# A four-layer network on one core: the convolution loop and the MLP on queries, with routing, put in the order of written tables, and the last group of queries in two halves

## The chip, the cores and the metric

The kernel runs on one core of a Trainium2 chip. Its engines are TensorE (PE), VectorE (DVE), ScalarE (ACT), GpSimd (POOL) and SyncE (SP); each works through its own queue in order, and semaphores tie the queues together. The metric is the device time of one execution in microseconds (us), the median of several runs; lower is better.

## The reference, cut to what matters

Four layers follow each other on 4096 tokens (8 sequences of 512) of 128 values, each on a layer norm of its input and added back to it:

```
x = x + conv(layernorm(x))      # running mean per sequence, 31 softmax weights per head and position, sum of 31 shifted copies, projection, norm
x = x + ffn(layernorm(x))       # block-quantised gated MLP, 128 -> 352 -> 128
x = x + ttt(layernorm(x))       # q, k, v; two steps of training of (gate, val, proj) on k, v; then the MLP on q:
                                #   o = (silu(q @ gate) * (q @ val)) @ proj @ proj_w + proj_b
x = x + moe(layernorm(x))       # 8 experts of 128 -> 512 -> 128, best 2 per token, at most 1229 tokens for an expert
```

For each token and each of its two choices, `moe` counts how many choices before it went to the same expert; that is its place, and a token beyond the last place is dropped for that choice. All first choices count ahead of all second ones.

## The kernel before

Tokens lie on the 128 partitions: 32 tiles of 128 tokens, in 8 groups of 4 tiles (512 tokens). Everything is float32, and a float32 matmul runs as two passes on PE. A scheduler puts the instructions of each engine in order by the order in which the program issues them and by what they depend on; where a program passes instructions through a `Line`, that engine keeps them in just the order of the calls.

**The convolution** (`sequence_conv`, 0 to 245 us) takes one sequence at a time, in a software pipeline over `cur`, `nxt`, `then` and `old` (this sequence, the next two and the one before). DVE, PE, ACT and part of POOL are passed through one `Line` each. The parts:

- `gate` and `tap`: matmuls `eg` and `ev` from the running means; ACT makes `sg` of `eg`. `energy`: two DVE operations, `en` and the running maximum `top`. `turn_top`, `greatest`, `turn_greatest`: `top` is turned on PE (`tt`), reduced on DVE (`mx`), widened on ACT (`mw`), turned back (`mb`); `less` takes it off the energies (DVE), and `weigh` makes the exponentials on ACT, a copy in PSUM (`w`) and one in SBUF (`en`) for each of four groups of taps.
- `part_sums`, `sums`, `invert`, `turn_inverse`: the softmax's sums by matmul (`pn`), a copy (`dn`, ACT), matmul (`sm`), reciprocal (DVE, L448), widened (`rw`, ACT), turned on PE (`rb`) and copied out (`rbs`, ACT). `tt`, `mb`, `pn`, `sm`, `rb` and the means `av` share one PSUM buffer.
- `shared` (POOL) and `product` (DVE, L483) multiply the weights with the shifted means, `add_up` sums them on PE (`cv`, L492), 8 matmuls for each of four groups.
- `scale_down`, `project`, `norm1`, `finish`, `add_beta`: scaling on DVE (`cs`), projection on PE (`pj`), statistics on DVE and the root on POOL, then ACT and POOL. `scaled` normalises the tokens of a later sequence (ACT), `means` makes its running means (PE, ACT, DMA).

The order in which the loop calls these parts is the order on every engine.

**The feed-forward part, training and Newton-Schulz** (245 to 930 us) are not touched.

**The MLP on queries and routing** (the last part of `ttt`, and `Moe.route`; 931 to 1057 us). For each group: `pa` and `pb`, eight matmuls of 512 columns into four PSUM buffers; Silu on ACT (`sw`); product on DVE (`ht`, L1317); the 32 output passes on PE (`o`, L1323); and the sum with the residual on DVE (`x`, L1327). `moe.route(g - 1)` is issued between a group's products and its outputs. It turns `x` on PE (`tp`, copied by ACT to `xt`), takes the statistics and a reciprocal root of 13 small DVE operations (statistics at L1671 and L1672, the root at L87 to L95), makes logits on PE (`both`, L1678), scales them (`lg`), picks the best two experts with DVE operations of 128x32 and smaller, counts places with two matmuls against a triangle and ones (`both`, L1715 and L1716), and ends with the row number `slot` (L1727) of each choice. Nothing here goes through a `Line`: the scheduler interleaves the group's products, the group before and its routing. Then POOL scatters rows to DRAM with eight indirect DMAs (L1732), one for each tile and choice: the second choices first, then the first choices, each of which waits until the second choices of the group before have landed, since second choices fill an expert's rows from the end and a first choice must win where they meet.

**The experts** (`Moe.experts`, 1058 us to the end) load their rows from DRAM (SP, L1787 and L1788) once all scatters have landed. Their first instruction on PE is the turn `tp` at L1816, their first activation a Gelu (L1834), for which ACT loads a table.

Of the kernel before, what the change touches and what calls it, by code (L numbers as in the profile page):

```python
# [1 line left out]

# [5 lines left out]
F32 = mybir.dt.float32  # L8
# [8 lines left out]
P = 128  # L17
# [112 lines left out]
def flat(ap):  # L130
    return ap.rearrange("p a b -> p (a b)")
# [17 lines left out]
def sequence_conv(cx):  # L149
# [20 lines left out]
    BUSY = 14  # L170
    with ExitStack() as st:
# [430 lines left out]
        add_up(cur, 3)  # L602
        for b in range(1, B):
            cur, nxt, then, old = seq[b], seq.get(b + 1), seq.get(b + 2), seq.get(b - 1)
            shared(cur)
            product(cur, 0)
            if b > 1:
                finish(seq[b - 2], nc.gpsimd)
            part_sums(cur)
            sums(cur)  # L610
            if old:
                scale_down(old)
                project(old)
            add_up(cur, 0)
            if nxt:
                for g in (2, 3):
                    energy(nxt, g)
            invert(cur)
            if nxt:
                turn_top(nxt)  # L620
            if then:
                gates(then, 0)
            product(cur, 1)
            if nxt:
                greatest(nxt)
            turn_inverse(cur)
            if then:
                taps(then, 0)
            if nxt:
                turn_greatest(nxt)  # L630
            add_beta(b)
            add_up(cur, 1)
            if old:
                norm1(old, nc.gpsimd)
            if b + 4 < B:
                scaled(b + 4)
            if b == B - 3:
                ffn.load(flat(tri)[:, : ffn.NW], cur["spread"])
            if b >= B - 2:
                last_weights(cur)  # L640
                shared(cur, NP, NGR)
            product(cur, 2)
            add_up(cur, 2)
            if then:
                for g in (0, 1):
                    energy(then, g)
                gates(then, 1)
                taps(then, 1)
            if nxt:
                less(nxt)  # L650
                weigh(nxt, 0, 1)
            if b + 3 < B:
                seq[b + 3] = means(b + 3)
            if nxt:
                weigh(nxt, 1, NGR)
            if b < B - 1:
                product(cur, 3)
                add_up(cur, 3)
# [253 lines left out]
def fp4_ffn(cx):  # L912
# [7 lines left out]
        "H0 G2 H1 x0 G3 P0 T0 s0 S0 A2 A3 t0 H2 H3 D0 C0 P1 S1 d0 c0 T1 U0 D1 C1 T2 C2 g0 "  # L920
        "R0 R0 W0 K0 U1 f0 O0 u0 a0 f1 f2 W1 g1 K1 W2 K2 a1 W3 E0 K3 f3 K4 K5 K6 R1 K7 R1 "
        "r0 O1 r0 o0 "
# [210 lines left out]
def ttt(cx):  # L1133
# [10 lines left out]
    with ExitStack() as st:  # L1144
# [148 lines left out]
        with ExitStack() as s4:  # L1293
# [10 lines left out]
            for g in range(NG):  # L1304
                ht = p2.tile([P, NF, W], F32, tag="ht", name="ht")
                for c in range(NF):
                    pa = ps_h.tile([P, W], F32, tag="h", name="pa")
                    nc.tensor.matmul(
                        pa, gate[:, c * P : (c + 1) * P], qt[:, g * W : (g + 1) * W], start=True, stop=True
                    )  # L1310
                    pb = ps_h.tile([P, W], F32, tag="h", name="pb")
                    nc.tensor.matmul(
                        pb, val[:, c * P : (c + 1) * P], qt[:, g * W : (g + 1) * W], start=True, stop=True
                    )
                    sw = p2.tile([P, W], F32, tag="sw", name="sw")
                    nc.scalar.activation(sw, pa, AF.Silu)
                    nc.vector.tensor_tensor(ht[:, c, :], pb, sw, ALU.mult)  # L1317
                if g:
                    moe.route(g - 1)
                o = ps_o.tile([P, G, D], F32, tag="o", name="o")  # L1320
                for j in range(G):
                    for c in range(NF):
                        nc.tensor.matmul(  # L1323
                            o[:, j, :], ht[:, c, j * P : (j + 1) * P], w2[:, c, :],
                            start=(c == 0), stop=(c == NF - 1),
                        )
                nc.vector.tensor_tensor(grp(cx.x, g), o, grp(cx.x, g), ALU.add)  # L1327
            moe.route(NG - 1)
# [254 lines left out]

class Moe:
# [66 lines left out]

    def route(self, g):
        cx = self.cx
        nc, tc, p2 = cx.nc, cx.tc, self.p2
        vec = nc.vector

        def small(tag, *shape, dt=F32):
            return p2.tile([P, *shape], dt, tag=tag, name=tag)

        def over_e(t):  # L1660
            return t.unsqueeze(2).to_broadcast([P, G, E])

        x, at = grp(cx.x, g), slice(g * G, (g + 1) * G)
        tp = self.ps_t.tile([P, G, P], F32, tag="t", name="tp")
        for j in range(G):
            nc.tensor.transpose(tp[:, j, :], x[:, j, :], cx.ident)
        xt = small("xt", G, P)
        nc.scalar.copy(xt, tp)
        st, mv = small("st", G, 6), small("mv", G, 2)
        for j in range(G):  # L1670
            vec.bn_stats(st[:, j, :], x[:, j, :])  # L1671
            vec.bn_aggr(mv[:, j, :], st[:, j, :])  # L1672
        rs, off = small("rs", G), small("off", G)
        rsqrt(nc, p2, mv[:, :, 1], 1e-5, rs, G)
        both = self.ps_r.tile([P, 4, G, E], F32, tag="r", name="both")
        pl, pos = both[:, 3], both[:, :3]
        for j in range(G):
            nc.tensor.matmul(pl[:, j, :], xt[:, j, :], self.w_c, start=True, stop=True)  # L1678
        lg = small("lg", G, E)
        vec.tensor_tensor(lg, pl, over_e(rs), ALU.mult)  # L1680
        vec.tensor_tensor(lg, lg, self.b_g.unsqueeze(1).to_broadcast([P, G, E]), ALU.add)
        vec.scalar_tensor_tensor(off, mv[:, :, 0], -1.0, rs, ALU.mult, ALU.mult)
        rows = [self.xr[:, k, at, :] for k in range(K)]
        for j in range(G):
            nc.scalar.activation(
                rows[0][:, j, :D], x[:, j, :], AF.Identity, bias=off[:, j : j + 1], scale=rs[:, j : j + 1]
            )

        hot, best, rk, tmp = small("hot", K + 1, G, E), small("best", K, G), small("rk", K, G), small("tmp", G, E)
        for k in range(K):  # L1690
            vec.tensor_reduce(best[:, k, :], lg, AX.X, ALU.max)
            vec.tensor_tensor(tmp, lg, over_e(best[:, k, :]), ALU.is_equal)
            vec.tensor_tensor(tmp, tmp, self.rank, ALU.mult)
            vec.tensor_reduce(rk[:, k, :], tmp, AX.X, ALU.max)
            vec.tensor_tensor(hot[:, k], self.rank, over_e(rk[:, k, :]), ALU.is_equal)
            if k + 1 < K:
                vec.scalar_tensor_tensor(flat(lg), flat(hot[:, k]), -1e30, flat(lg), ALU.mult, ALU.add)
        vec.tensor_copy(hot[:, K], hot[:, K - 1])

        dif = small("dif", G)  # L1700
        vec.tensor_tensor(dif, best[:, 0, :], best[:, 1, :], ALU.subtract)
        nc.scalar.activation(dif, dif, AF.Tanh, scale=0.5)
        for k, s in enumerate((0.5, -0.5)):
            vec.tensor_scalar(rows[k][:, :, D + 1], dif, s, 0.5, ALU.mult, ALU.add)

        vec.tensor_copy(rows[1][:, :, :D], rows[0][:, :, :D])
        cum = small("cum", K + 1, G, E)
        vec.tensor_copy(cum[:, :K, 0, :], self.seen)
        for j in range(1, G):
            vec.tensor_tensor(cum[:, :K, j, :], cum[:, :K, j - 1, :], hot[:, :K, j - 1, :], ALU.add)  # L1710
        vec.tensor_tensor(self.seen, cum[:, :K, G - 1, :], hot[:, :K, G - 1, :], ALU.add)
        vec.tensor_tensor(
            cum[:, K], cum[:, K - 1], self.seen[:, 0:1, :].to_broadcast([P, G, E]), ALU.add
        )
        nc.tensor.matmul(pos, self.before, hot, start=True, stop=False)  # L1715
        nc.tensor.matmul(pos, self.ones, cum, start=False, stop=True)  # L1716
        vec.tensor_tensor(cum, pos, hot, ALU.mult)
        r = small("r", K + 1, G)
        vec.tensor_reduce(r, cum, AX.X, ALU.add)
        room = small("room", K, G)  # L1720
        vec.tensor_scalar(room, r[:, ::2, :], float(CAP), None, ALU.is_lt)

        vec.tensor_scalar(r[:, 1, :], r[:, 1, :], -1.0, CAP - 1.0, ALU.mult, ALU.add)
# [6 lines left out]
        for k in (1, 0):  # L1730
            for j in range(G):
# [7 lines left out]
                if k == 0 and g:  # L1739
                    self.after(sc, self.scatters[-1][:G])  # L1740
# [180 lines left out]
```

## Time and profile before

| what | value |
|---|---|
| time, median of 3 runs | 1241.89 us (1241.77 to 1242.49) |
| the profiled execution's own time | 1242.03 us |
| its span | 1240.3 us, 15590 instructions |
| PE busy | 1097.9 us (89%) |
| DVE busy | 754.0 us (61%) |
| ACT busy | 488.0 us (39%) |
| POOL busy | 736.8 us (59%) |

A row of the timeline has the start and the duration in us, the engine, the line, the operation, the tile that is written and those that are read, the shape, and in brackets how long the engine had stood idle and what ended that. "L1327" is line 1327 of the kernel before. A row of the waits has the total in us, the number of waits and the longest. A matmul's record covers several passes, and its end is modelled; durations overlap a little, so distances from start to start are the better measure of what an instruction takes of its engine.

### The profile page before, as it was taken

To read this page: it belongs to the slowest core of one execution; us is meant where nothing else is said; L and a number is where in the kernel's file an instruction comes from. 1 tells how busy PE (TensorE), PEld (TensorE's weight loads), DVE (VectorE), ACT (ScalarE), POOL (GpSimd) and SP (SyncE) were. 2 spreads that over 40 slices of the span, in tenths; PEclk is the share of its full clock that TensorE was granted. 3 is DMA by queue.
4 is the path that set the end of the run, shared out by engine and by line. 5 is a ranking of instruction groups with operands and counts; after the bars stand their busy time and mean duration, and the time that the engine had idled before them with its cause. 6 is when DMAs were issued, how large, how long until landed. Compare 5 with 4: busy or idle time off the path is not lost.

```text
span 1240.3 us, 15590 instructions
## 1 busy us (share of the span) xinstructions
PE 1097.9 (89%) x5335; PEld 661.5 (53%) x5335; DVE 754.0 (61%) x1788; ACT 488.0 (39%) x1001; POOL 736.8 (59%) x720
## 2 busy tenths in 40 slices
PE   6999997858987899999988999999899993799992
PEld 4343432536666455555566455555576762577772
DVE  6899999988986544444455444444466785123354
ACT  4656554335657322232244232222343331243331
POOL 2266667635656888888822888888400656255553
PEclk9999999878999899999999999999999997799996
DMA  5324435860000000000000000000000111221277
GB/s 155 90 85 118 119 97 192 318 196 2 1 1 1 1 1 1 1 0 1 1 1 1 1 1 0 1 1 1 1 1 1 44 44 45 59 72 50 68 193 208
DMA packets 66894, 67.27 MB, mean 54 GB/s; under 512 B 6927, under 2 KB 48734, under 8 KB 66816
## 3 DMA queue, kind: packets, MB, share of 16 engines
q1 hardware_dynamic: 59296, 56.57, 15.3%
q0 software_dynamic: 4608, 8.43, 2.1%
q10 hardware_dynamic: 2912, 1.29, 0.4%
q8 instruction: 42, 0.69, 0.2%
q14 instruction: 36, 0.29, 0.1%
HBM read 40.00 MB, written 27.13 MB: 54 GB/s over the span
## 4 chain that ended last, share of the span: by engine, by line
PE 58%; DVE 21%; ACT 9%; issue 4%; POOL 3%; DMA 3%; ACTq 0%; DVEq 0%; POOLq 0%; SPq 0%
PE ph L1537 5%; PE sum L1512 5%; PE po L1844 4%; PE pp L1527 4%; PE sum L1511 4%; PE sum L1513 4%; PE ph L1831 4%; PE pa L1489 4%; PE pb L1491 4%; DVE v L858 3%; PE cv L492 2%; DVE pr L483 2%; PE pt L1520 2%; PE gu L974 1%; DVE ht L1317 1%
## 5 line engine op out<-in xcount | busy, mean ns | idle before, releaser
L1502 POOL TENSOR_TENSOR ds<-sw,s 128x512 f32<-128x512 f32 x64 | 81.7, 1276 | 86.3 <-DVE sw L1497 86.3
L1504 POOL TENSOR_TENSOR ds<-ds,s 128x512 f32<-128x512 f32 x64 | 111.6, 1744 | 5.0
L1732 POOL DMA_INDIRECT rows<-xr,slot x64 | 62.9, 983 | 73.8 <-DVE rs L95 45.1
L1495 ACT COPY b<-pb 128x512 f32<-128x512 f32 x64 | 37.5, 586 | 162.1 <-PE pb L1491 161.5
L1858 POOL DMA_INDIRECT res<-ye,xe x60 | 58.4, 974 | 66.2 <-DVE ye L1856 28.1
L472 POOL TENSOR_TENSOR pr<-base,en 128x512 f32<-128x512 f32 x52 | 74.9, 1474 | 36.9 <-ACT en L428 36.5
L1499 DVE TENSOR_TENSOR h<-sw,b 128x512 f32<-128x512 f32 x64 | 50.2, 785 | 70.6 <-ACT b L1495 70.1
L1834 ACT ACTIVATE ht<-ph,b 128x512 f32<-128x512 f32 (+2 forms) x100 | 56.1, 588 | 93.5 <-PE ph L1831 92.0
L483 DVE TENSOR_TENSOR pr<-base,w 128x3072 f32<-128x3072 f32 (+2 forms) x27 | 86.3, 3206 | 0.8 <-ACT w L426 0.8
L1503 POOL TENSOR_TENSOR ds<-sw,ds 128x512 f32<-128x512 f32 x64 | 82.8, 1294 | 5.0
L1505 POOL TENSOR_TENSOR ds<-ds,b 128x512 f32<-128x512 f32 x64 | 81.6, 1274 | 5.0
L1527 PEld LDWEIGHTS pp<-proj,ht 128*128 128x128 f32 x512 | 67.1, 191 | 30.7 <-issue 29.8
L1844 PE MATMUL po<-w,ht 128*128 128x128 f32 (+1 forms) x640 | 77.8, 278 | 0.0
L1522 ACT COPY ht<-pt 128x512 f32<-128x512 f32 x64 | 37.6, 587 | 101.5 <-PE pt L1520 101.5
L1497 DVE TENSOR_TENSOR sw<-pa,s 128x512 f32<-128x512 f32 x64 | 44.2, 691 | 53.7 <-ACT s L1493 53.7
L1831 PE MATMUL ph<-xt,w 128*128 128x512 f32 (+2 forms) x200 | 73.4, 511 | 3.4 <-DVE xt L1819 3.4
L1844 PEld LDWEIGHTS po<-w,ht 128*128 128x128 f32 (+1 forms) x640 | 74.6, 189 | 0.7
L1539 DVE TENSOR_TENSOR db<-ph,sw 128x512 f32<-128x512 f32 x64 | 44.2, 691 | 47.2 <-PE ph L1537 47.2
L1537 PE MATMUL ph<-proj_t,dpt 128*128 128x512 f32 x128 | 71.6, 641 | 0.0
L492 PE MATMUL cv<-pr,sel 128*32 128x512 f32 x512 | 62.4, 616 | 8.6 <-DVE pr L483 8.6
L1489 PE MATMUL pa<-gate,kt 128*128 128x512 f32 x128 | 66.8, 604 | 2.5 <-ACT b L1495 2.4
L1512 PE MATMUL sum<-db,k 128*128 128x512 f32 x128 | 66.2, 598 | 1.6 <-DVE db L1539 1.6
(359 smaller groups left out, 2545.6 us busy)
## 6 DMA issues: line engine op xcount, KB each, us to landing
base<-far SPq DMA_DIRECT2D x64, 268.0 KB, 5.2
rows<-empty SPq DMA_DIRECT2D x1, 5005.0 KB
res<-zero SPq DMA_DIRECT2D x1, 4096.0 KB, 26.3
own<-zero SPq DMA_DIRECT2D x2, 2048.0 KB, 18.8
w<-in_L_ffn_W SPq DMA_DIRECT2D x16, 256.0 KB, 4.8
y<-res SPq DMA_DIRECT2D x16, 256.0 KB, 5.5
xe<-rows SPq DMA_DIRECT2D x7, 585.0 KB, 4.3
y<-own SPq DMA_DIRECT2D x12, 256.0 KB, 4.7
```

Of the source, the lines that this page charges most:

```text
L483: vec(nc.vector.tensor_tensor(s["pr"][g][:, lo:hi, :], s["base"][:, lo:hi, at], w.to_broadcast([P, hi - lo, L]), ALU.mult))
L492: ten(nc.tensor.matmul(s["cv"][32 * j : 32 * (j + 1), :], sel[:, i].rearrange("p a h -> p (a h)"), s["pr"][g][:, i * NJ + j, :], start=(g ...
L1489: nc.tensor.matmul(pa, ki, gate, start=True, stop=True)
L1502: nc.gpsimd.tensor_tensor(ds, sw, s, ALU.mult)
L1503: nc.gpsimd.tensor_tensor(ds, sw, ds, ALU.subtract)
L1504: nc.gpsimd.tensor_tensor(ds, ds, s, ALU.add)
L1505: nc.gpsimd.tensor_tensor(ds, ds, b, ALU.mult)
L1512: nc.tensor.matmul(sums[1], ki, db, **kw)
L1527: nc.tensor.matmul(pp, ht[:, c * P : (c + 1) * P], proj[:, c, :], start=(c == 0), stop=(c == NF - 1))
L1537: nc.tensor.matmul(ph, dpt, proj_t, start=True, stop=True)
L1831: ten(nc.tensor.matmul(ph[:, :n], self.w1[:, e, c * P : (c + 1) * P], xt[:, :n], start=True, stop=True))
L1844: ten(nc.tensor.matmul(po[:m, i - lo, :], ht[:, c, (i - lo) * P : (i - lo) * P + m], self.w2[:, e, c, :], start=(c == 0), stop=(c == NF - ...
```

## The change

**The loop of the convolution** is written as a table of parts and a string that gives their order, for all sequences alike. A part is named by a letter and called with a number; one whose sequence does not exist is skipped. On the engines these things move: `finish` stands behind `part_sums` and `sums`; the reciprocal (`invert`) between the two energies of the next sequence; `add_up` of group 1 directly behind its product, ahead of `rb` on PE; `greatest` behind `norm1`; `turn_inverse` and its copy `rbs` behind `scaled`; `add_beta` behind `norm1`; the weights of group 3 are made ahead of those of group 2.

**The MLP on queries** runs DVE, PE and ACT through a `Line` each, in the order of two strings: one for all groups with a successor, one for the last. The eight groups become nine: seven of four tiles and two of two tiles. In the round of a group, the routing of the group before is spread between its products in steps (`Route`), so that its slots and scatters come in the same round; in the last round the routing of both halves alternates. The first pair of matmuls of the next group stands at the end of a round.

Within routing, three DVE operations go to ACT: the copy of the rows for the second choice (128x512, L1706 before), the copy of `hot` (L1698) and the two weights (L1704). The logits share the PSUM buffer of the turn. The wait of each first-choice scatter becomes one small memset on POOL (`gate`), which waits for the second choices of the group before, and behind which the first choices stand in order. Last, an activation on one column (`ahead`) asks for the Gelu table when routing has ended.

```diff
+    ORDER = (
+        "S0 P0 D0 n0 N0 F0 J0 e2 A0 v0 e3 t0 g0 g1 P1 A1 Z0 L0 X0 T0 P2 s0 i0 k0 k1 m0 B0 A2 E0 E1 g2 g3 "
+        "k2 k3 l0 w0 M0 w1 w3 w2 p3 a3 "
+    )
...
-            shared(cur)
-            product(cur, 0)
-            if b > 1:
-                finish(seq[b - 2], nc.gpsimd)
-            part_sums(cur)
-            sums(cur)
...
+            for name in ORDER.split():
+                at, part = parts[name[0]]
+                if at is not None:
+                    part(at, int(name[1]))
...
-            for g in range(NG):
-                ht = p2.tile([P, NF, W], F32, tag="ht", name="ht")
...
-                if g:
-                    moe.route(g - 1)
...
-            moe.route(NG - 1)
+            ORDER = (
+                "a2 t0 a4 H1 u0 a2 S1 l0 b1 G0 b8 H2 S2 b4 G1 b1 H3 n0 S3 n1 n2 n3 m0 c7 G2 c1 d4 G3 O0 "
+                "O1 d3 e6 v0 O2 O3 f6 x0 f2 h0 s0 "
+            )
+            LAST = (
+                "a1 H1 S1 t0 u0 a6 G0 H2 S2 a1 l0 b9 b4 G1 b1 H3 c1 S3 n0 n1 G2 c1 n2 n3 m0 G3 c2 O0 O1 "
+                "c4 d1 x0 T0 U0 d1 A1 d1 A1 d1 A2 d3 L0 e1 B1 e1 B1 e1 B1 e3 v0 B5 f1 B2 f1 B1 f1 B1 f1 "
+                "B1 f1 B1 N0 N1 C1 f1 C1 f2 C1 M0 C5 D7 E4 V0 F8 "
+            )
+            vec, ten, act = Line(tc), Line(tc), Line(tc)
+            parts = [(g * G, G) for g in range(NG - 1)] + [(NT - G, G // 2), (NT - G // 2, G // 2)]
...
+            ahead = wp.tile([P, 1], F32, tag="ahead", name="ahead")
+            act(nc.scalar.activation(ahead, cx.eps[1e-5], AF.Gelu_apprx_tanh))
...
+        new = []
+        for k in (1, 0):
+            if k == 0 and lo:
+                gate = nc.gpsimd.memset(self.small("gate", 1), 0.0)
+                m.after(gate, m.scatters[-1][: len(m.scatters[-1]) // K])
+            for j in range(n):
+                sc = nc.gpsimd.indirect_dma_start(
...
+                if k == 0 and lo:
+                    after(tc, sc, gate, sync=False)
...
-                if k == 0 and g:
-                    self.after(sc, self.scatters[-1][:G])
```

In the second string, `H` is a pair of matmuls, `S` its Silu, `G` its product, `O` the outputs of a tile, `x` the sum; `t`, `u`, `l`, `m`, `v`, `n` are the turn, its copy, the logits, the copy of rows, the matmuls of the places and the normalised rows of the group before; `a` to `f` followed by a number are so many steps of its statistics, root, first choice, second choice, counts and slots, the scatters being the last step of `f`. `h` and `s` are the first pair of the next group and its Silu, and capitals in the last string belong to the last half.

## The prediction

> **What bounds the kernel now.** Two stretches are touched, so each was read for itself. For the convolution loop (66 to 230 us) the waits of VectorE (DVE) come first: the loop looks DVE-bound, and these are its only gaps.
>
> ```profile
> DVE rs L448 <- PE sm L444: 2.7, 4, 2.2
> DVE mx L405 <- PE tt L400: 2.2, 4, 0.6
> ```
>
> Columns: total us, times, longest. In the timeline the sequences in the middle of the loop repeat every 26.34 us (`sm` at 97.05, 123.39, 149.72) with 0.16 and 0.55 us of these waits in each, so DVE works 25.63. What repeats is a chain on TensorE (PE) and ScalarE (ACT) that DVE only follows: sm 123.39, projections, cv, `tt`, eg at 128.61; four sg, `mw` and `rbs` on ACT until 133.25; `mb` 133.31; two groups of cv (3.57); eg at 137.46; then av, the exponentials, pn, dn and 12.26 later the next sm.
>
> For the queries, the busy time by stretches (columns: stretch, length, then PE, PEld, DVE, ACT, POOL busy, granted clock, DMA share, GB/s):
>
> ```profile
> 1012.00:1026.00 14.00, 13.39 (x66) 8.65 (x66) 11.17 (x63) 5.32 (x11) 8.80 (x10) 1.00 0.12 39
> 1026.00:1040.00 14.00, 8.06 (x61) 6.98 (x59) 10.26 (x65) 4.36 (x11) 9.27 (x10) 0.90 0.15 49
> 1040.00:1061.00 21.00, 1.48 (x4) 1.00 (x4) 3.86 (x23) 0.41 (x2) 13.29 (x14) 0.50 0.20 60
> ```
>
> PE bounds the groups; after the last group it stands for 17.75 us while routing ends. The timeline says on what:
>
> ```profile
> 1019.26 0.68 DVE L1327 TENSOR_TENSOR x<-o,x 128x512 f32<-128x512 f32 x1
> 1032.48 0.68 DVE L1327 TENSOR_TENSOR x<-o,x 128x512 f32<-128x512 f32 x1
> ...
> 1036.54 0.17 DVE L1727 TENSOR_SCALAR slot<-rk 128x8 int32<-128x8 f32 x1 [0.24 <-DVE sq L93]
> 1036.98 0.97 POOL L1732 DMA_INDIRECT rows<-xr,slot  x1 [2.29 <-DVE rs L95]
> ...
> 1045.16 0.17 DVE L1727 TENSOR_SCALAR slot<-rk 128x8 int32<-128x8 f32 x1 [0.18 <-DVE rk L1725]
> 1047.34 0.97 POOL L1732 DMA_INDIRECT rows<-xr,slot  x1 [0.31 <-DMA rows<-xr,slot]
> ...
> 1056.28 0.97 POOL L1732 DMA_INDIRECT rows<-xr,slot  x1 [0.30 <-DMA rows<-xr,slot]
> 1058.70 0.93 SPq L1787 DMA_DIRECT2D xe<-rows  x2
> 1061.41 1.08 PE L1816 MATMUL tp<-ident,xe 128*128 128x128 f32 x4 [17.75 <-DMA xe<-rows]
> ```
>
> Sums of group 6 at 1019.26, its slots 17.3 us later; then 16 scatters of 1.275 us each in one unbroken row on GpSimd (POOL): the last eight have slots at 1045.33 but start at 1047.34. The expert stage starts 4.16 us after the last scatter ends (1057.25). So the stretch to price is sums of group 6 to last scatter: 37.99 us.
>
> **Convolution loop, part by part.** DVE runs the same operations. (1) add_up of group 1 (8 matmuls, 1.74) stands ahead of `rb` instead of behind `mb`. Before, PE waited 0.53 for `mb` and then did two cv groups. Now eg ends at 130.35, cv 132.09, rb 132.5, ev 134.5. In sequences 1 to 3 the four `scaled` activations (1.52) stand ahead of `rbs`, so `mb` goes from 133.31 to 134.83, one cv group follows, and eg comes at 137.19: 0.27 earlier. In 4 and 5 nothing is scaled, `mb` comes at 134.5, eg at 136.9: 0.57 earlier. The sums of sequence 5 come 3 x 0.27 + 0.57 = 1.38 earlier. (2) On DVE the reciprocal L448 stands ahead of the second energy pair (0.77 + 0.90 = 1.67): what is queued behind its wait is that pair and the next product. The pair was run while DVE would wait; now it runs after. (3) `mx` goes behind the statistics, by when `tt` is ready: 0.55 gone. From sequence 5 on DVE sets the pace, so 1.38 - 1.67 + 0.55 = 0.26 earlier. (4) `finish` moves behind dn on ACT: dn starts at 122.74, 0.17 after pn ends, so pn held it, nothing gained. The order of weights 3 and 2 leaves the last exponential in place. The beta addition behind norm1 on POOL has POOL's 7 us of idle time in each sequence as cover; without it it would cost its 1.28. Sequence 7 keeps its 2.25 wait. Ends: the whole 1.95 of the PE side (3 x 0.27 + 2 x 0.57) gained, or PE gaining nothing, 1.67 - 0.55 = 1.12 lost. I take 0.26.
>
> **Queries: one group.** PE work stays: eight 512-column matmuls of two passes (0.86 each), 6.9; 32 output passes at 0.1115, 3.6; logits 0.9, turns 0.45, positions 0.45: 12.3 us, where sums were 13.1 to 13.2 apart (979.81, 992.95, 1006.08, 1019.26). Now routing of the group before stands in DVE's order between the four gated products, in one chain. By starts, from the sums x: statistics at 0.81 (as 1019.26 to 1020.04); eight of these, 1.2; rs and first product at 2.08, 0.61; twelve root operations at 0.20 (L93 to L95 in the timeline), 2.4; second product 4.97; off and logits at 5.68, seven operations at 0.223 (L1680 to L1695); third product 7.1; five more; fourth product at 8.7. Before, PE resumed 0.73 after the start of the fourth product, so at 9.43; behind it 26 passes (2.9) and the positions (0.4), and the sums start 0.2 later: a round of 12.95. PE waits some 0.8 in each at the fourth product, which is less than it lost before, and everything else (positions at 10.6, POOL's 8 x 1.275) fits.
>
> First sums: fourth product 938.12 + 0.73 + 2.9 + 0.25 = 942.0. Group 6: 942.0 + 6 x 12.95 = 1019.7, 0.44 later than now, because the first rounds were short (11.85, 12.72).
>
> **Queries: the end, from group 6's sums.** The first half's round: products of 256 columns (0.32 apart) bring the fourth product to 7.8, positions to 9.85, and with six operations at 0.2 to 0.29 the first half's sums to 11.2 and group 6's slots to 11.7 (now 17.3). Scatters from 11.95: 8 x 1.275 and a gate, to 22.5. The gate is a new wait on POOL, with four scatters queued behind: its condition was met 5 us before, so it costs its memset (`seen` L1649, 0.11) and an issue gap (0.30), 0.4; its lower end is 0.
>
> Second half, from 11.2: four statistics 1.1, first product 0.3, 13 roots to 3.9, second product. Its fourth pair of matmuls waits for that product's buffer (4.3 to 5.15), so the fourth product comes at 5.35 and the half's sums at 7.1. Two chains then alternate at 0.10 to 0.12 (as at 1035.17 to 1036.14): slots of the first half at 11.9; then the second half alone, logits to slot 23 operations at 0.2, and positions at half clock (0.74, as at 1042.92): slots at 17.3. That is 11.2 + 17.3 + 0.1 = 28.6, and POOL is through with the first half's four scatters at 11.2 + 11.9 + 0.2 + 5.5 = 28.8. The last four (5.1) and a gate (0.4), less the gap of 0.3 that closes the row: end at 34.0. Against 37.99 that is 4.0 earlier, less the 0.44: 3.56.
>
> A 128x2 root operation is not in the trace. 128x12 takes 0.17, 128x4 0.16: so 0.08 if it went by size, 0.16 if size does not matter; I take 0.16, the nearest row. At 0.08 the second half's slots would come 2 us earlier, and POOL would still hold the end at 34.0.
>
> [...] No row of this trace shows a 128x2 operation.
>
> [...]
>
> `ahead` loads the Gelu table early. Before, the load took 1.28 at 1065.56, but the fourth expert matmul of half clock ended only at 1069.2 and ACT waited for it: 0 gained, 1.28 at most. PE still idles some 12 us ahead of the experts, so the slow matmuls (0.85 a pass until 1067.8) stay.
>
> **Sum.** Profiled run: 1242.03 (span 1240.3). Less 0.26 and 3.56: 1238.2; the median is 0.14 under the profiled run, so 1238.1.
>
> **Rivals.** *Nothing comes of it.* Four small waits per round that a chain in one order can't fill (x to statistics, logits, positions, fourth product, 0.1 each) make the round 13.35. Six rounds later that is 2.4 more: 1240.5. For it: DVE was 11.2 busy of 14 with two chains interleaved; now they stand one behind the other. Against: every step above is a start-to-start distance, waits included.
>
> *Slower: DVE becomes the bound.* In some stretches a root operation followed after 0.28 rather than 0.20 (1010.36 to 1010.64 L91 to L93). If the 24 dependent operations ahead of the fourth product took 0.07 more, the round is 14.6, and six rounds give 10.1 more: 1248.2. It decides from a round of 12.95 + 3.82 / 6 = 13.6. Against: those 0.28 had another chain's operation in between.
>
> *The loop loses.* If `mb` behind four activations delays cv beyond PE's gain, the loop loses 1.12 instead of gaining 0.26: 1239.5, at the edge of faster.
>
> *More than said.* Rounds near PE's 12.3 take off 6 x 0.65 = 3.9 more: 1234.2.
>
> **How the numbers follow.** Forecast (1235.5 to 1239.5, the loop's loss in it) 0.62; nothing 0.20; slower 0.13; more 0.05. One measurement tells 0.2%, 2.5 us, from no change: under 1239.4 is faster. That gives faster 0.66 (0.62, 0.05, less a little at the edge), same 0.20, slower 0.14. Range: 1235.0 to 1243.0, which leaves out most of the slower case and the better half of the last.
>
> **What would show it.** Sums `x` about 12.95 apart from the second group on; group 6's slots about 12 us after its sums; the last scatter ending near 1053.5; the PE wait for the experts' rows at 11 to 13 us; in the loop no wait at `mx`, one of about 0.4 at the reciprocal, period 26.1. Rounds over 13.6, or a last scatter after 1057, would make the prediction wrong, as would a loop that moves by over 2 us.

## The result, and the profile after

The changed kernel takes 1254.96 us (median of 5 runs, 1253.95 to 1257.54), the kernel before 1241.9 beside it: 1.0105 times the time, interval 1.0094 to 1.0117. It is slower by 13 us; 1238.1 was predicted.

The runs of this study stood on several chips. Where before takes 1242 to 1244 us, all is as above. On two others before takes 1274; there the query rounds of the changed code are slower too (last section), while the stages ahead of the queries take the same on all (901.6 to 903.2 us from the first `sm` to the first query sums, wherever the loop has the order of before). So times are compared only with those on the same chip, and the loop by distances inside a profile. These are from the profiled runs, start to start in us:

| stage | before | after | two moves back (e7) |
|---|---|---|---|
| first `sm` (sequence 0) to last `sm` (sequence 7) | 181.94 | 192.37 | 182.96 |
| last `sm` to the first query sums | 720.67 | 724.20 | 720.64 |
| first query sums to those of group 6 | 76.78 | 78.73 | 78.71 |
| group 6's sums to the end of the last scatter | 37.99 | 35.39 | 33.81 |
| group 6's sums to the first expert matmul | 42.15 | 39.90 | 38.37 |
| first expert matmul to the end | 178.89 | 176.95 | 177.54 |

The 13.96 us of the first two rows are the loss; the queries and the end give 2.24 back (297.82 to 295.58). That leaves 11.7 of the 12.9 between the times of the two profiled runs; 0.6 lie ahead of the first `sm` and 0.6 outside the spans. The profile names the kind of loss in its row of the granted clock (40 slices of 31 us; 9 is 90% or more). First before:

```profile
PEclk9999999878999899999999999999999997799996
```

and after:

```profile
PEclk8999888878999999999999999999999998799997
```

Slices 5 to 7 lie in the convolution loop: it ran at full clock and now runs at 0.8 to 0.9. The waits of DVE in the loop (66 to 235 us; total us, times, longest), after:

```profile
DVE rs L453 <- PE sm L449: 8.5, 5, 2.5
DVE en L394 <- PE ev L362: 3.8, 4, 1.1
DVE mx L410 <- PE tt L405: 0.9, 1, 0.9
```

The wait at `mx` went, as said, but for one of 0.9. The one at the reciprocal was to be 0.4 a sequence beside sequence 7's 2.25; it is 0.61 in the one sequence that no lower clock touches, 1.55 to 2.12 in three others and 2.48 in sequence 7, 8.5 in all, because PE is late with `sm`. What PE does around `sm` shows in its timeline (start, length, instruction; in brackets the idle time ahead of it and who ended it). Before:

```profile
120.91 1.66 PE L434 MATMUL pn<-en,sel 128*32 128x512 f32 x4 [0.29 <-ACT en L428]
123.39 1.06 PE L444 MATMUL sm<-fold,dn 128*128 128x16 f32 x8 [0.83 <-ACT dn L439]
124.30 0.47 PE L504 MATMUL pj<-xn,ident 128*128 128x128 f32 x2
```

After:

```profile
153.04 1.05 PE L439 MATMUL pn<-en,sel 128*32 128x512 f32 x4 [0.90 <-ACT en L433]
154.77 1.06 PE L449 MATMUL sm<-fold,dn 128*128 128x16 f32 x8 [0.69 <-ACT dn L444]
156.18 0.49 PE L509 MATMUL pj<-xn,ident 128*128 128x128 f32 x2 [0.34 <-ACT v L528]
...
156.79 0.64 PE L509 MATMUL pj<-xn,ident 128*128 128x128 f32 x2
```

PE stands 1.93 us in three pieces within 4 us, where it stood 1.12 in two; and in the middle of `pj` a pair goes from 0.49 to 0.64: the clock has dropped. It drops for whole stretches of 3.41 us: the records of the granted clock in the trace last multiples of 3.413 us. Cutting the span at those marks (columns: stretch, length, PE busy, granted clock, DMA share, GB/s) gives, after:

```profile
149.82:153.24 3.42, 2.52 (x18) 1.00 0.71 227
153.24:156.65 3.41, 2.38 (x16) 1.00 0.99 275
156.65:160.06 3.41, 3.41 (x19) 0.50 0.79 225
```

and before:

```profile
122.50:125.91 3.41, 2.58 (x23) 1.00 1.03 251
125.91:129.33 3.42, 3.42 (x26) 1.00 0.90 213
```

The window in which PE is busy for 2.38 us is followed by one at half clock, which costs 1.7 us of PE time (half of 3.41); those with 2.52 and 2.58 are not. Between 66 and 200 us of the 18 profiled runs there are 657 windows that begin at full clock: of 612 with at least 2.45 us busy none is followed by a halved one, of 45 with less 26 are. The other 19 are told apart by `sm`: its eight matmul passes have only 16 columns each, yet the profile counts 1.06 us of busy time for them. In the two windows above, `sm` alone, first after, then before:

```profile
153.24:156.65 3.41, 1.06 (x8) 1.00 0.99 275
122.50:125.91 3.41, 1.06 (x8) 1.00 1.03 251
```

That leaves 1.32 us of other work in the window that is followed by half clock, and 1.52 in the one that is not. The kernel before also has windows with less than 2.38 us busy that are not followed by half clock. Its next sequence has this one, with only one pass of `sm` in it (first all of PE, then `sm` alone):

```profile
146.39:149.80 3.41, 2.30 (x8) 1.00 0.95 270
146.39:149.80 3.41, 0.07 (x1) 1.00 0.95 270
```

Without `sm`, each of the 26 windows that are followed by half clock has at most 1.41 us busy, and each of the 631 others at least 1.43. This split was read from the same windows that it sorts, and its edge is narrow; in the rest of the kernel, where other matmuls run, the two kinds overlap (ahead of 66 us between 1.42 and 1.59).

Between the first `sm` and the last, before has one halved window, after eight: 7 x 1.7 is 11.9, and the loop lost 10.4. What the 3.5 between the last `sm` and the first query sums are was not taken apart. The periods of the loop tell the same as the windows. Where no window is halved the sequence takes 26.13 us (26.38 before; 26.07 predicted), with one 28.07, with two 29.32.

For the queries, the busy time by stretches:

```profile
1028.00:1042.00 14.00, 12.79 (x75) 9.93 (x73) 11.62 (x62) 6.64 (x19) 8.78 (x10) 1.00 0.14 44
1042.00:1056.00 14.00, 10.75 (x55) 9.24 (x56) 10.70 (x59) 5.23 (x16) 8.94 (x11) 0.88 0.14 44
1056.00:1075.00 19.00, 3.02 (x14) 2.29 (x13) 7.90 (x58) 4.36 (x14) 10.91 (x13) 0.55 0.19 57
```

and the end in the timeline:

```profile
1035.75 0.69 DVE L1333 TENSOR_TENSOR x<-o,x 128x512 f32<-128x512 f32 x1 [0.52 <-PE o L1325]
...
1048.46 0.42 DVE L1333 TENSOR_TENSOR x<-o,x 128x256 f32<-128x256 f32 x1
1048.80 0.16 DVE L1766 TENSOR_SCALAR slot<-rk 128x8 int32<-128x8 f32 x1
...
1065.42 0.17 DVE L1766 TENSOR_SCALAR slot<-rk 128x4 int32<-128x4 f32 x1
...
1065.94 0.14 POOL L1771 MEMSET gate<- 128x1 f32 x1
1066.35 0.97 POOL L1774 DMA_INDIRECT rows<-xr,slot  x1 [0.26 <-issue]
...
1070.17 0.97 POOL L1774 DMA_INDIRECT rows<-xr,slot  x1 [0.30 <-DMA rows<-xr,slot]
...
1075.65 1.09 PE L1927 MATMUL tp<-ident,xe 128*128 128x128 f32 x4 [11.51 <-DMA xe<-rows]
```

In a group PE is busy for 12.79 of 14 us (13.39 before). Group 6's slots come 13.05 us after its sums instead of 17.28; PE waits 11.51 for the experts' rows instead of 17.75.

### The profile page after: what moved, and what is told of

Read it like the earlier page. It is cut to its first block, busy times and chain, and to the rows that moved or that the text cites. A ratio compares the mean times of both kernels' runs of the same rounds, so it can differ in the third digit from the quotient of the medians.

```text
span 1252.6 us, 15664 instructions
## 1 busy us (share of the span) xinstructions
PE 1112.0 (89%) x5355; PEld 677.3 (54%) x5355; DVE 763.0 (61%) x1798; ACT 498.2 (40%) x1044; POOL 738.9 (59%) x728
## 4 chain that ended last, share of the span: by engine, by line
PE 53%; DVE 16%; ACT 3%; POOL 3%; issue 3%; DMA 2%; POOLq 0%; DVEq 0%; SPq 0%; ACTq 0%
PE ph L1577 5%; PE sum L1552 5%; PE pp L1567 4%; PE sum L1551 4%; PE sum L1553 4%; PE po L1955 4%; PE pa L1529 4%; PE ph L1942 4%; PE pb L1531 4%; DVE v L842 3%; PE o L1325 2%; PE pt L1560 2%; DVE ht L1318 2%; PE gu L957 1%; DMA y<-own 1%
## 5 line engine op out<-in xcount | busy, mean ns | idle before, releaser
L497 PE MATMUL cv<-pr,sel 128*32 128x512 f32 x512 | 66.2, 639 | 9.5 <-DVE pr L488 9.4
```

## Experiments

Two theories: *clock* (PE stands too long within one window around pn, sm and pj; the halved window that follows is the loss) and *order* (the moves made the chain longer; the clock follows). The letters are those of the table in the change; in the loop's, `S` is `shared`, `P` and `p` `product`, `A` and `a` `add_up`, `n` and `N` `part_sums` and `sums`, `F` `finish`, `D` and `J` `scale_down` and `project`, `v` and `i` `invert` and `turn_inverse`, `e` and `E` energies, `t`, `T` and `m` `turn_top`, `greatest` and `turn_greatest`, `g` and `k` `gate` and `tap`, `l` `less`, `w` the exponentials, `Z` `norm1`, `B` `add_beta`, `s` `scaled`, `M` the means.

**e1, e11: the loop's old order.** Queries and routing stay changed.

```diff
-S0 P0 D0 n0 N0 F0 J0 e2 A0 v0 e3 t0 g0 g1 P1 A1 Z0 L0 X0 T0 P2 s0 i0 k0 k1 m0 B0 A2
+S0 P0 F0 n0 N0 D0 J0 A0 e2 e3 v0 t0 g0 g1 P1 T0 i0 k0 k1 m0 B0 A1 Z0 s0 L0 X0 P2 A2
...
-w0 M0 w1 w3 w2 p3 a3
+w0 M0 w1 w2 w3 p3 a3
```

> The table of the convolution loop is put back to the order of the kernel before; queries and routing stay changed. Both theories: the loop is 14.5 us shorter again (first query sums near 942.5) and the queries keep what they gained, 297.8 - 295.6 = 2.2 us from the first query sums to the end: 1239.7. If the query part had lost time unseen: 1242 or more. If the time lost ahead of the queries does not come from the loop's table at all: 1254 to 1256.

> The loop's order of before with the changed queries and routing, a second time, since its first run stood on a chip where before took 1273.7 us. Both theories: 2.2 to 3 us under before, 1239 to 1241 where before takes 1242 to 1243; the better of all orders of the loop so far, so under the 1241.7 of the kernel with two moves undone.

Measured 1252.4 and 1251.9, where before took 1273.7 and 1274.8 (0.9828, interval 0.9811 to 0.9844, and 0.9826, 0.9812 to 0.984). From the first `sm` to the first query sums 902.55 and 903.21 (before 902.61, after 916.57). The loss comes from the table. The times expected were for chips where before takes 1242, and were missed.

**e2, e8, e9: idle matmuls in the pause, order untouched.**

```diff
             for g in range(NGR):
+                for _ in range(2 if g == 2 and s["b"] else 0):
+                    ten(nc.tensor.matmul(
+                        pn[32 * g : 32 * (g + 1), :], sel[:, 0].rearrange("p a h -> p (a h)"), s["en"][:, 0, :],
+                        start=True, stop=True,
+                    ))
                 ten(nc.tensor.matmul(
```

e2 had three with 128 columns of `cx.ident`, e8 four with 512, e9 two.

> The changed kernel, its order untouched, with three idle 128-column matmuls (0.65 us) between the second and third partial sum (pn) of each sequence but the first, where TensorE stood still for 0.90 us; their output is overwritten. Clock theory (the loop loses because the clock is granted at half for 4 us after TensorE stood still too long around pn, sm and pj): most of the halved stretches in the loop vanish and the time falls to 1240 to 1247. Order theory (the chain itself got longer by the moves, the clock is a by-product): 1255 to 1257, the added matmuls coming on top.

> The changed kernel, order untouched, with four idle 512-column matmuls (0.43 us each) between the second and third partial sum; the three of 128 columns tried first ran beside the partial sums in another strip of columns and filled nothing, TensorE still stood 0.90 us. Clock theory: the window that holds pn is busy 0.9 us longer (2.2 becomes about 3), most halved stretches of sequences 1 to 4 go and the time falls by 5 to 12 us. Order theory: 0 to 3 us slower than the changed kernel.

> The changed kernel, order untouched, with two idle 512-column matmuls between the second and third partial sum. The four of the run before kept the clock up to 183 us but took 0.86 each in their strip of columns and made a sequence 28.0 us long without any halving; two should fit into the 1.95 us between the second partial sum's start and the third's. Clock theory: no halved stretch before 180 us, sequences of 26.1 to 26.4 us, time 1241 to 1248 where the changed kernel takes 1254. Order theory: 1254 to 1257.

e2: 1265.3 (0.9934 of before's 1273.7); the three matmuls ran beside the partial sums in another strip of columns (as in e9's timeline, where an idle one starts at 122.26 beside partial sums that run from 122.24 to 122.84), PE still stood 0.90, and the halved windows stayed: 916.86 us from the first `sm` to the first query sums. It tells nothing apart. e8: 1263.9 (1.0168, 1.0151 to 1.0185). No window of the loop was halved up to 183 us, but the sequences took 27.6 to 28.0: four are two too many. The time I expected was wrong, the clock right. e9: 1260.7 (0.9894 of 1274.8), with 911.22 from the first `sm` to the first query sums (after 916.57). In the four periods from the second `sm` on, where the pause is, it has one halved window instead of four:

```profile
96.74:100.16 3.42, 2.70 (x14) 1.00 0.86 240
124.05:127.46 3.41, 2.38 (x15) 1.00 0.89 264
127.46:130.88 3.42, 3.42 (x20) 0.50 0.83 242
```

They take 26.06, 26.54, 28.12 and 26.13 us, where the changed kernel takes 26.13, 28.07, 29.32 and 27.72: 4.4 less, with the same order and two matmuls more. That is against the order theory. Its "no halving before 180" was missed by the window of 2.38 us, in which sm's and pj's pauses still lie. Outside these four sequences the idle matmuls cost time: the period ahead of them is 31.61 instead of 30.80, the two behind them are 28.82 and 23.83 (27.12 and 23.21 in the changed kernel), so that the whole loop is only 1.26 shorter.

**e3, e4, e7: one small move undone, the other, both.**

```diff
-w0 M0 w1 w3 w2 p3 a3
+w0 M0 w1 w2 w3 p3 a3
...
-S0 P0 D0 n0 N0 F0 J0
+S0 P0 D0 F0 n0 N0 J0
```

> The changed kernel with the exponentials in order 1, 2, 3 again instead of 1, 3, 2, nothing else. Clock theory: the wait of TensorE ahead of the third partial sum goes from 0.90 back to 0.29, halved stretches get fewer, 1240 to 1248. Order theory (reciprocal ahead of the energies, or eight matmuls ahead of rb, is the cost): 1254 to 1256.

> The changed kernel with the finish of the sequence two back ahead of the partial sums again (its four activations ahead of dn on ScalarE), nothing else. The wait of pj for v (0.34 a sequence) goes. Clock theory: the pause of 0.90 + 0.69 stays, so a part of the halved stretches stays; 1243 to 1254. Order theory: 0.34 x 6 = 2 us at most, 1253 to 1255.

> The changed kernel with two of the loop's moves undone: the exponentials in order 1, 2, 3 and finish ahead of the partial sums. The other moves stay (eight matmuls ahead of rb, reciprocal ahead of the energies, mx behind the statistics, beta behind norm1). Clock theory: the window of 3.41 us that holds pn, sm and pj is then busy for about 2.6 us as before, not 1.8 to 2.4, no halving before 195 us, periods of 26.1 us where the first pauses leave the clock alone; first query sums at 941 to 943 and the time 12 to 15 us under the changed kernel. Order theory: less than 3 us under the changed kernel.

e3: 1261.3 (0.9898 of 1273.7); first `sm` to first sums 910.24, six halved windows up to the last `sm` instead of eight. e4: 1259.2 (0.9869), 910.91, also six. Each alone takes back about half of the 13.0 that both take back. e7: 1241.7 beside before's 1243.2 (0.9989, 0.9979 to 0.9998) and 1254.2 of the changed kernel; 903.60, and the windows with pn and sm are as before:

```profile
122.96:126.37 3.41, 2.59 (x20) 1.00 1.01 286
174.16:177.57 3.41, 2.59 (x16) 1.00 0.97 269
```

The large moves (eight matmuls ahead of rb, the reciprocal ahead of the energies) do not cause the 13 us by themselves; that they make the small ones dearer shows in e10. They bring nothing either: the loop is 1.0 us longer than before's (182.96 against 181.94). Sequences 1 to 4 take 26.28, 26.15, 26.41 and 25.75 us, where before takes 26.34 to 26.38, but sequence 5 takes 25.88 instead of 24.37. There PE, ahead by a cv group, stands 2.90 us for the product on DVE (1.30 before), and a halved window follows.

**e5, e6: both kernels once more.**

> The kernel before, unchanged, profiled beside the next three, because it took 1273.7 us beside the first four runs and 1241.9 beside the changed kernel. If a stage is slower there whatever the kernel, the profile shows which: expected in the queries, where rounds of the first runs were 14.4 us after a first one of 13.0. The convolution loop should stay at 26.34 us a sequence and no halved clock before 214 us.

> The changed kernel, unchanged, timed beside the same runs of before. Clock theory: again about ten halved stretches in the convolution loop and 14 us more than before up to the first query sums. If the loss were a matter of one chip or of the moment, the halved stretches would be gone and the loop at 26.1 us a sequence.

e5 stood on a chip where before takes 1243.2, so it does not show what is slower on the others: 1245.4, 182.0 in the loop, one halved window in it. e6: 1254.2 (1.0086, 1.0069 to 1.0103), eight halved windows, 916.34. The loss is no matter of one run or chip.

**e10, e13, e14: on the old order, both small moves, the exponentials alone, finish alone.**

> The loop's order of before with only the two small moves: exponentials in order 1, 3, 2, and finish behind the partial sums. Queries and routing as in the changed kernel. Clock theory: the pauses at pn, sm and pj add up again, halved stretches appear in most sequences, 8 to 13 us more than with the loop's order of before beside it. If the large moves (eight matmuls ahead of rb, reciprocal) are needed for the halving: within 2 us of it.

> The loop's order of before with the exponentials in order 1, 3, 2 as its only move; queries and routing changed. The two moves together gave periods of 28.0 to 28.2 us in sequences 2 and 4 and 5 us more up to the first query sums. If the pause at pn alone (0.90 instead of 0.29, with 0.82 at sm) is enough: halved stretches in at least two sequences, first query sums 2 to 6 us later than with the loop of before (903 us after the first sm). If it needs finish's pause at pj as well: within 1 us of 903.

> The loop's order of before with finish behind the partial sums as its only move. A pause of about 0.34 at pj joins those of 0.29 at pn and 0.69 at sm: 1.3 us in all against 1.1 before and 1.93 in the changed kernel. If the clock goes by the time that TensorE stands in the window of 3.41 us, this stays on the safe side (window busy about 2.5): no halving before 195 us and 903 us from the first sm to the first query sums, within 1 us. If finish's place is a cause by itself: 2 us or more later.

e10: 1258.6 (0.9892 of 1274.8), 907.62 to the first sums, 4 to 5 more than with the old order: less than expected, and less than the 13.0 that the same two moves cost beside the large ones. Sequences 2 and 4 have a halved window and take 28.17 and 28.04. Sequence 3 stands as long (1.83 us busy, as ahead of sequence 4), is not halved and takes 26.72: its window ends after two passes of `sm`, those of sequences 2 and 4 hold all eight and seven. So the same pauses cost more or less by where the windows fall. e13: 1245.8 (1.0018, 1.0007 to 1.0028), 906.96. Sequences with no halved window take 26.38 and 26.33 as before, the two others 27.97 and 29.57: the order of the exponentials costs nothing but the clock.

```profile
123.42:126.83 3.41, 1.70 (x8) 1.00 0.94 276
126.83:130.24 3.41, 3.41 (x17) 0.50 1.04 297
130.24:133.66 3.42, 3.42 (x20) 0.50 0.22 61
```

e14: 1244.8 (1.0012, 1.0002 to 1.0022), 907.31: within 1 us was expected, so a miss. `pj` waits for `v`, and this is on the path: sequences without a halved window take 26.70 instead of 26.34. One window came to 2.39 and was halved (28.32):

```profile
126.33 0.76 PE L509 MATMUL pj<-xn,ident 128*128 128x128 f32 x2 [0.34 <-ACT v L528]
```

**e12, e16: idle matmuls ahead of the experts,** on the kernel of e11.

```diff
                 tp = ps_t.tile([P, W], F32, tag="t", name="tp")
                 n = 0
+                for _ in range(9 if (e, lo) == (0, 0) else 0):
+                    ten(after(tc, nc.tensor.matmul(tp, cx.ident, self.w1[:, 0, :W], start=True, stop=True), cx.last, sync=False))
```

`cx.last` is the last matmul of the positions, behind which the nine stand.

> As the kernel before this one, with nine idle 128x512 matmuls (0.86 us each at full clock, 1.7 at half) behind the last routing position, while TensorE waits 11.5 us for the experts' rows at half clock; their output is overwritten. Clock theory: the clock is back when the rows come and the first expert matmuls run at 0.43 instead of 0.85 a pass: 1.7 to 3.4 us under the kernel before this one. If the experts' first matmuls are not what the end waits for: no difference.

> The best version so far (loop's order of before, queries and routing changed, nine idle matmuls ahead of the experts) once more, for a ratio on another chip. It was 2.2 us under the same kernel without the idle matmuls. Where before takes 1242 to 1243: 1237 to 1238.5. Where before takes 1274: 1248 to 1251.

e12: 1249.65 beside e11's 1251.89; the ranges (1247.9 to 1250.4, 1251.5 to 1252.7) don't meet. In e11's timeline the first experts' matmuls took 1.08 and 5.74 us (in the kernel before, where the granted clock is 0.50 until 1068.0, 1.08 and 6.00):

```profile
1072.67 1.08 PE L1927 MATMUL tp<-ident,xe 128*128 128x128 f32 x4 [11.33 <-DMA xe<-rows]
1074.69 5.74 PE L1942 MATMUL ph<-xt,w 128*128 128x512 f32 x8 [0.94 <-DVE xt L1930]
```

in e12's 0.63 and 3.70, behind the nine idle ones, which stand as 18 passes:

```profile
1059.50 10.19 PE L1928 MATMUL tp<-w,ident 128*128 128x512 f32 x18
1071.20 0.63 PE L1930 MATMUL tp<-ident,xe 128*128 128x128 f32 x4 [1.52 <-DMA xe<-rows]
1072.77 3.70 PE L1945 MATMUL ph<-xt,w 128*128 128x512 f32 x8 [0.94 <-DVE xt L1933]
```

e16: 1238.9 beside before's 1243.8 (0.9958, 0.9946 to 0.9971): the fastest version.

**e15: without the early table load.**

```diff
-act(nc.scalar.activation(ahead, cx.eps[1e-5], AF.Gelu_apprx_tanh))
+act(nc.scalar.activation(ahead, cx.eps[1e-5], AF.Identity))
```

> The loop's order of before, queries and routing changed, but without the early load of the Gelu table (the activation ahead of the experts is an identity). The prediction put the load at nothing: then within 0.5 us of the kernel with it. If it was on the path: 1.28 us more.

1242.0 (0.9979, 0.9967 to 0.9992). From group 6's sums to the first expert matmul 38.25, from there to the end 177.40 (e14, with the load, on the same chip: 38.33 and 177.35). The kernel with the load and this loop was not timed there; by the distances the load was worth nothing, as predicted.

## Why the prediction was wrong

**The step that failed** is part (4) of the convolution loop: `finish` behind dn, "nothing gained", and the order of the exponentials, which "leaves the last exponential in place". Both sentences look at when a wait ends and take the clock of the trace, 1.00, as given. The last exponential did stay in place, but PE now had nothing to do for 0.90 us ahead of it; and `pj` waits for `finish` (its `v`), which the sum left out: 0.34 us, on the path. Together they pushed the window around `sm` from 2.59 us busy to between 1.8 and 2.4, and without `sm` from 1.52 to between 1.1 and 1.35: three gaps of 0.90, 0.69 and 0.34 us, each far shorter than the window of 3.41. The term of 0.26 gained became 10.4 lost in the loop and 3.5 behind it. The sign to watch for ("a loop that moves by over 2 us") was named; its mechanism was in no rival. "The loop loses" had the side and a tenth of the size.

**Right in the loop:** the one undisturbed sequence takes 26.13 (26.07 predicted), and in e7, where the clock leaves sequences 1 to 4 alone, no wait at `mx` is left. Not right: the size of both sides. In e7 the `sm` of sequence 5 comes 0.8 earlier (counted from the first `sm`) instead of 1.38, and that sequence takes 1.5 more: DVE's products begin 1.0 later in it, behind the reciprocal and the second energy pair, and the rest lies behind them, where the halved window is. In all the loop of e7 loses 1.0, near the prediction's lower end of 1.12 and not the 0.26 gained.

**Queries.** The round was 12.95, measured 13.12: six rounds cost 1.0 more. The end was sized well: in e7, where no window is halved until 21 us after group 6's sums, first half's sums come at 11.29 (11.2 predicted), second half's 6.91 later (7.1), and the last scatter is over at 33.81 (34.0). In the changed kernel a halved window at 1044 to 1048 us makes the first and the last of these 12.71 and 35.39. Where the windows fall decides this: of the eight profiled runs with the changed queries on the faster chips, four have a halved window there and end at 35.1 to 35.4, four have none and end at 33.8. The 128x2 root operations (L1678) took 161 ns on average, those of 128x4 164, so between these two size made no difference, and the 0.16 taken from the nearest row holds. In routing the trace before had 128x2 only as the aggregate of the statistics (L1672, 141 to 182 ns), which reads 128x6. With the copy of L1706 on ACT no scatter of routing but the first takes over 1.0 us; before, of the seven beside the copy four took 1.04 to 1.11 and three 0.97. The gate was priced too high: three of the last four run while POOL waits for slots, and the last one stands in a pause that was there anyway, so that its two scatters start 1.35 apart (1065.00 and 1066.35) instead of 1.275: 0.08, not 0.4. The experts take 176.95 us where before takes 178.89; this was not predicted, but it is not clear of the spread either (176.3 to 179.0 in the profiled runs with the changed queries and no idle matmuls, 178.1 and 178.9 in the two of before).

## What to carry to other kernels

TensorE's pauses had a price of their own here: of the 45 windows with less than 2.45 us of work 26 were followed by half clock, of the 612 others none. Before a reorder of such a loop, add up how long TensorE works within any 3.4 us, not only who ends last, and leave passes like those of `sm`, of 16 columns, out of that sum. Here the danger began under 1.43 us of such work in 3.41, and the kernel before had 1.52 around `sm`: it ran 0.1 us from the edge, which no row of its waits shows. Where TensorE waited 11.3 us, idle matmuls that ended 1.52 us before the data came gained 2.2 us (e12); where they were more than the pause, four of 512 columns in one of 0.90, a sequence took 27.6 to 28.0 us with no halved window instead of 26.13 (e8).

## What the runs showed of the hardware

On the two chips where before takes 1274 us, the query rounds of the changed code take 14.2 to 14.6 us from the second on instead of 13.1. The wait for the positions grows from 5.3 to 18.6 us in all; the line shown for e11 is the largest part of it. In e7 (before 1243) and then e11 (before 1275), DVE's waits in the queries:

```profile
DVE cum L1759 <- PE pos L1753: 5.3, 8, 0.8
```

```profile
DVE cum L1759 <- PE o L1325: 9.8, 4, 2.5
```

With the same instructions DVE goes on as soon as the positions are there on the one chip (waits of at most 0.8), and on the other in four rounds only when PE's next sixteen matmuls are through (waits of 2.4 to 2.5). The cause is open. Before was not profiled there, so where its 31 us go was not shown; but against it the kernel of e2, the changed one with matmuls that filled nothing, was 0.7% faster there. The verdict of slower holds for the chips where before takes 1242 to 1244.
